# A new tail, split last stores and new places in a two-layer adjacency residual-norm kernel on one core

## Chip, core and metric

The kernel runs on one core of a Trainium2 chip. The metric is the device time of one execution in microseconds (us). Before the change it is 2085.56 us, the median of 3 runs (2084.93 to 2086.3). About 0.2% of it, 4.2 us, is what a measurement of this kernel can tell from no change.

## What is computed

There are 128 batches; each has x (128 x 512) and an adjacency matrix adj (128 x 128), all in float32. Two layers follow each other, and each ends in a residual and a layer norm.

```
# layer 0
agg = (adj @ x) / max(rowsum(adj), 1e-6)
x   = layernorm(x + relu(concat(x, agg) @ W.T))
# layer 1
Xw  = x @ Wv + bv;  sj, si = Xw @ aw[:d], Xw @ aw[d:]
A   = adj * exp(leaky_relu(sj[None, :] + si[:, None] + ab, 0.2))
T   = A / (rowsum(A) + 1e-12)
H   = sum over k = 0, 1, 2 of (T^k x) @ Wk[k] + bk[k]
x   = layernorm(x + relu(H))
```

## The kernel before

The 128 batches are worked in 32 groups of G = 4, first all groups in layer 0 (stage A), then all groups in layer 1 (stage B). The large products x @ W are made by a fast 2 x 2 block scheme with seven products in place of eight, with block sums of x and of the weights made beforehand.

**Chains and steps.** Every piece of TensorE work is a step of a chain, written as a name and a number.

- Stage A: chains P12, P56 and P74 (`pair`, line 305, seven steps of two 128x256 products each) and T (`last`, line 388, eleven steps: seven 128x256 products, then four 128x512 products with the turned adjacency).
- Stage B: chains O1, O2, O5, O6, O7, O4, O3 (`outer`, line 617, seven steps of one 128x385 product each) and C (`combine`, line 812). C has eight steps: for each batch b a `one(b)`, T times a 512-column row, and a `two(b)`, which adds T times another row on top. In C the steps are one(0), one(1), one(2), two(0), one(3), two(1), two(2), two(3).

A float32 product is two passes on TensorE. One `mm` (line 155) is one product. A step of a chain of seven usually waits on VectorE (DVE), ScalarE (ACT) or GpSimd (POOL) work that empties or refills a PSUM bank. For example step 3 (`prod(X, 6)`) is followed by DVE making W = X + s5 (line 637 in stage B), and step 5 (`prod(X, 7)`) writes X again and so must wait for that addition. In the T chain DVE lines 400 and 401 read what step T.2 left in the upper half of a bank, and T.3 writes the same bank.

**Order.** Two lanes of four PSUM banks each (bA0 to bA3, bB0 to bB3) hold two chains at a time. The order in which their steps alternate is written out by hand in strings: PA for a group of stage A, PT and PG for the passage from A to B, PB for a group of stage B, PL for the last group (lines 855 to 865). Everything else (loads, block sums on POOL, the turns `x_turn` at line 259 on DVE, layer norm, softmax pieces, stores) is put between the steps by tables PLACES_S, _A, _B, _M, _L and _T, which give each operation a position in half steps (lines 915 to 1027). Each engine runs its own instructions strictly in that order, so a waiting instruction holds up what is queued behind it on its engine. Nearly all DMAs are issued by SyncE (SP), in order too.

**Weights of the T matrix in stage B.** For all groups but the last, the 128x512 row of scores is sent through DRAM and turned. The last group is handled apart, so that nothing has to go to DRAM at the end:

- `t_scores` (line 721) makes dg, diagonal matrices of the scores, and `end_scores` (746) multiplies a matrix of ones by dg, takes the leaky relu and exp on ACT.
- `end_rows` (756): for each half h (two batches), DVE multiplies by the adjacency (760), and TensorE multiplies ones by T, a 128x256 product that leaves the row sums in every partition.
- `end_norm` (763): DVE adds epsilon (768), takes a 128x256 reciprocal (769) and multiplies T by it (770).
- The chain C of the last group: one(b) makes a product, DVE makes v1 from it in two additions (829, 830), ACT copies the addend of the second product into the same bank (831), two(b) multiplies on top, and DVE adds the residual (380).
- Layer norm of the last group: batches 0 and 1 by ACT squares and POOL (`end_mean`, `end_var`, `end_scales`), batches 2 and 3 by DVE `bn_stats` and POOL (`end_stats`, `end_rstd`); `end_apply` runs on ACT for batches 0 and 1, on DVE (565) for 2 and 3. `end_store` (569) has SP store each batch, 256 KB, in one DMA.

At the start, eight 128x512 products with the identity (lines 151 and 152) run on the eight banks while the first loads land.

Of the kernel before, what the change touches and what calls it, by code (L numbers as in the profile page):

```python
# [8 lines left out]
FP = mybir.dt.float32  # L9
# [7 lines left out]
def kernel(  # L17
# [41 lines left out]
    def need(*keys):  # L59
        for k in keys:  # L60
            assert k in done, k
# [89 lines left out]
    for t in bA + bB:  # L151
        nc.tensor.matmul(t, ident, ident[:, None, :].to_broadcast([P, Q, P]), start=True, stop=True)
# [414 lines left out]
    def end_store(b):  # L567
        need(("end_apply", b))
        nc.sync.dma_start(out[(NG - 1) * G + b], ys[2 * NG - 1, b // 2][:, b % 2])
# [186 lines left out]
    def end_rows(g, h):  # L756
        need(("end_scores", g), ("adj_turn",))
        T = TTs[g][:, 2 * h : 2 * h + 2].rearrange("p b n -> p (b n)")
        pt = lanes[0][1 + h][:, :FH]
        V.tensor_mul(T, T, adjs[2 * NG - 1][:, 2 * h : 2 * h + 2].rearrange("p b n -> p (b n)"))  # L760
        mm(pt, ones[:].to_broadcast([P, P]), T, True)

    def end_norm(g, h):
        need(("end_rows", g, h))
        T = TTs[g][:, 2 * h : 2 * h + 2].rearrange("p b n -> p (b n)")
        pt = lanes[0][1 + h][:, :FH]
        rr = halves()[:, :FH]
        V.tensor_scalar(rr, pt, ROW_EPS, None, ALU.add)
        V.reciprocal(rr, rr)  # L769
        V.tensor_mul(T, T, rr)  # L770
# [41 lines left out]
    def combine(lane, g):  # L812
        n = NG + g
        X, Y, W, Z = lane
        at_ = {0: X, 1: Z, 2: W, 3: Y}
# [8 lines left out]
        def one(b):  # L824
            need(("end_norm", g, b // 2) if g == NG - 1 else ("t_turn", g))
            need(("O4" if b > 1 else "O3", g, 7), ("sum_c", g, 0), ("sum_c", g, 1))
            mm(at_[b], TTs[g][:, b], row(b, 0, F, 0), True)
            v = v1[b] = v1s[(g * G + b) % 3]
            V.tensor_add(v[:, :258], at_[b][:, :258], row(b, F, 2 * BW, 0))
            V.tensor_add(v[:, 258:], at_[b][:, 258:], row(b, 0, 254, 1))  # L830
            L_.copy(at_[b], row(b, 254, 766, 1))  # L831

        def two(b):
            mm(at_[b], TTs[g][:, b], v1[b])
            late.append((residual, n, b, at_[b]))
# [15 lines left out]
    def step(lane, name, g, k):  # L851
# [3 lines left out]
    PA = "p74.5 P12.1 P12.2 p74.6 P12.3 p74.7 P12.4 t.1 P12.5 P12.6 t.2 P12.7 P56.1 t.3 P56.2 t.4 t.5 P56.3 t.6 t.7 t.8 t.9 t.10 t.11 P74.1 P74.2 P56.4 P56.5 P56.6 P74.3 P56.7 P74.4".split()  # L855
    PT = "p74.5 p74.6 O1.1 O1.2 O1.3 p74.7 O1.4 t.1 O1.5 O1.6 t.2 O1.7 O2.1 t.3 O2.2 t.4 t.5 O2.3 t.6 t.7 t.8 t.9 t.10 t.11 O2.4 O2.5 O2.6".split()
    PG = ("O5.1 O5.2 O5.3 O5.4 O2.5 O2.6 O6.1 O6.2 O5.5 O5.6 O5.7 O7.1 O6.3 O6.4 O7.2 "
          "O6.5 O2.7 O7.3 O6.6 O7.4 O6.7 O4.1 O4.2 O7.5 O4.3 O7.6 O7.7 O4.4 c.1 O4.5 "
          "O4.6 c.2 c.3 c.4 O4.7 O3.1 O3.2 O3.3 O3.4 c.5 c.6 c.7 c.8 O3.5 O3.6").split()
    PB = ("O1.1 o3.7 O1.2 O1.3 O2.1 O1.4 O1.5 O1.6 O2.2 O1.7 O2.3 O2.4 O5.1 O5.2 O2.5 O5.3 O2.6 O5.4 O2.7 "  # L860
          "O6.1 O5.5 O6.2 O5.6 O6.3 O5.7 O6.4 O7.1 O6.5 O6.6 O7.2 O7.3 O6.7 O4.1 O7.4 O7.5 O4.2 O4.3 O7.6 "
          "O4.4 O4.5 O7.7 c.1 O4.6 O4.7 O3.1 O3.2 c.2 O3.3 c.3 c.4 c.5 c.6 c.7 c.8 O3.4 O3.5 O3.6").split()
    PL = ("O1.1 o3.7 O1.2 O2.1 O1.3 O2.2 O1.4 O1.5 O1.6 O1.7 O2.3 O2.4 O5.1 O2.5 O5.2 O2.6 O2.7 O5.3 O5.4 O6.1 O5.5 O6.2 "
# [44 lines left out]
    def place_op(n, pos, name, m, *a):  # L908
# [3 lines left out]
        else:  # L912
# [3 lines left out]
        ("ln_apply", -2, 3): 4, ("ln_var", -2, 0): -9, ("sum_c22", -2): -40, ("ln_scales", -2): -1, ("ln_mean", -2): -15,  # L916
        ("ln_var", -2, 2): -4, ("load_y", -2, 1): -27, ("ln_apply", -2, 2): 10, ("ln_var", -2, 1): -4,
        ("load_y", -2, 0): -31, ("x_s4", -1): -36, ("ln_var", -2, 3): -12, ("x_s1", -1): -66, ("a_load", -2): -65,
        ("a_turn", -2): -36, ("x_s3", -1): -52, ("y_store", -2, 1): 25, ("ln_apply", -2, 1): 15, ("x_turn", 0, 0, 1): -20,
        ("y_store", -2, 0): 32, ("ln_apply", -2, 0): 15, ("load_left", 0, 0): -49, ("ln_apply", -1, 3): 68, ("x_s2", 0): 28,  # L920
        ("x_turn", 0, 1, 1): -37, ("load_adj", 0): 154, ("ln_var", -1, 0): 58, ("sum_c22", -1): 21, ("ln_scales", -1): 62,
        ("ln_mean", -1): 48, ("x_turn", 0, 0, 0): -28, ("ln_var", -1, 2): 55, ("load_y", -1, 1): 38, ("load_y", -1, 0): 40,
        ("ln_var", -1, 1): 55, ("ln_apply", -1, 2): 70, ("x_s1", 0): 5, ("x_turn", 0, 1, 0): -39, ("a_load", -1): 7,
        ("x_turn", 1, 0, 1): 55, ("x_inner", 0, 0): -12, ("a_norm", -1): -23, ("ln_var", -1, 3): 58, ("degree", -1): -48,
        ("a_turn", -1): 27, ("x_s3", 0): 19, ("y_store", -1, 1): 95, ("ln_apply", -1, 1): 79, ("x_inner", 0, 1): -29,
        ("y_store", -1, 0): 100, ("ln_apply", -1, 0): 82, ("load_left", 1, 0): 9, ("x_s1", 1): 97, ("x_turn", 1, 0, 0): 41,
        ("x_s2", 1): 99, ("x_s4", 0): 80, ("load_left", 1, 1): -24, ("x_inner", 1, 1): 61, ("x_turn", 1, 1, 0): 32,
        ("x_s3", 1): 127, ("x_inner", 1, 0): 64, ("x_turn", 1, 1, 1): 47, ("x_s2", -1): -44,
    }
    PLACES_A = {  # L930
        ("x_s4", 0): 35, ("ln_apply", 0, 3): 131, ("x_s2", 1): 86, ("x_turn", 1, 1, 1): 33, ("ln_var", 0, 0): 124,
        ("sum_c22", 0): 87, ("ln_scales", 0): 126, ("w_slot", 0, 1): 24, ("ln_mean", 0): 113, ("x_turn", 1, 0, 0): 33,
        ("ln_var", 0, 2): 124, ("load_y", 0, 1): 100, ("ln_var", 0, 1): 118, ("load_y", 0, 0): 100, ("ln_apply", 0, 2): 134,
        ("x_s1", 1): 67, ("x_turn", 1, 1, 0): 28, ("a_load", 0): 73, ("x_inner", 1, 0): 51, ("a_norm", 0): 36,
        ("ln_var", 0, 3): 115, ("degree", 0): 17, ("load_left", 2, 1): 38, ("w_slot", 0, 0): 4, ("a_turn", 0): 90,
        ("x_s3", 1): 83, ("y_store", 0, 1): 157, ("ln_apply", 0, 1): 140, ("x_turn", 1, 0, 1): 42, ("x_inner", 1, 1): 36,
        ("load_adj", 1): 37, ("y_store", 0, 0): 161, ("ln_apply", 0, 0): 138, ("load_left", 2, 0): 78,
    }
    PLACES_B = {
        ("t_norm", 0): 154, ("sum_r", 0, 1): 81, ("load_y", 0, 0): 170, ("ln_var", 0, 3): 230, ("x_turn", 1, 0, 1): 19,  # L940
        ("t_back", 0): 165, ("x_s1", 1): 66, ("ln_scales", 0): 239, ("t_sums", 0): 149, ("x_turn", 1, 1, 1): 19,
        ("load_left", 2, 0): 82, ("ln_var", 0, 1): 227, ("y_store", 0, 0): 264, ("t_turn", 0): 187, ("ln_var", 0, 2): 224,
        ("sum_c", 0, 0): 109, ("ln_apply", 0, 2): 273, ("ln_apply", 0, 3): 257, ("x_inner", 1, 1): 53, ("ln_var", 0, 0): 235,
        ("t_exp", 0): 140, ("load_left", 2, 1): 70, ("ln_apply", 0, 1): 257, ("y_store", 0, 1): 278, ("x_s2", 1): 68,
        ("x_turn", 1, 1, 0): -5, ("x_s3", 1): 97, ("ln_apply", 0, 0): 242, ("t_load", 0): 123, ("t_scores", 0): 119,
        ("x_turn", 1, 0, 0): 14, ("sum_r", 0, 0): 86, ("x_s4", 0): 42, ("load_adj", 0): 103, ("load_y", 0, 1): 190,
        ("ln_mean", 0): 223, ("sum_c", 0, 1): 115, ("x_inner", 1, 0): 41,
    }
    PLACES_M = {
        ("ln_mean",): 212, ("ln_apply", 3): 234, ("ln_var", 1): 219, ("ln_apply", 0): 250, ("y_store", 0): 251,  # L950
        ("ln_apply", 2): 231, ("ln_var", 2): 225, ("ln_apply", 1): 235, ("ln_var", 3): 225, ("ln_scales",): 230,
        ("y_store", 1): 244, ("ln_var", 0): 227,
    }
    PLACES_L = {
        ("end_store", 2): 158, ("sum_c", 1): 72, ("sum_r", 0): 71, ("end_store", 0): 158, ("t_scores",): 105,
        ("end_var", 1): 134, ("sum_r", 1): 71, ("load_adj",): 96, ("load_y", 0): 47, ("end_apply", 1): 160,
        ("load_y", 1): 106, ("end_mean", 1): 128, ("end_rows", 0): 111, ("end_mean", 0): 127, ("end_rstd", 2): 132,
        ("end_store", 1): 160, ("end_apply", 2): 137, ("end_stats", 2): 129, ("end_store", 3): 162, ("end_scales",): 140,
        ("sum_c", 0): 76, ("end_rstd", 3): 149, ("end_apply", 0): 144, ("end_scores",): 106, ("end_rows", 1): 111,
        ("end_norm", 0): 111, ("end_stats", 3): 138, ("end_norm", 1): 111, ("end_apply", 3): 158, ("adj_turn",): 96,  # L960
        ("end_var", 0): 131,
    }
    OPS = {f.__name__: f for f in (load_left, load_y, load_adj, x_turn, x_inner, x_s1, x_s2, x_s3, x_s4, sum_c22, degree, a_norm, a_load, a_turn, w_slot, ln_mean, ln_var, ln_scales, ln_apply, y_store, sum_r, sum_c, t_scores, t_load,
           t_exp, t_sums, t_norm, t_back, t_turn, end_scores, end_rows, end_norm)}
# [115 lines left out]
```

## Time and profile before

| | |
|---|---|
| median of 3 runs | 2085.56 us |
| the profiled execution's own time | 2083.08 us |
| its span, first to last instruction | 2081.3 us |
| TensorE matmul (PE), share of the span | 99% |
| TensorE weight loads (PEld), in parallel to PE | 64% |
| DVE / ACT / POOL | 73% / 56% / 66% |
| granted TensorE clock, mean | 0.998 |
| chain that ended last | 97% PE |
| DMA | 287.13 MB, mean 138 GB/s |

A line of the timeline is: start in us, length in us, engine, line, operation, out<-in with shapes, how many were merged (x), and in brackets how long the engine had been idle and who ended that. The wait table says which engine and line waited for which, in total us, times, and the longest. Ends of matmuls are modelled: a matmul's line is longer than the distance to the next, and a short stall shows only as a larger distance between starts.

### The profile page before, as it was taken

What the parts mean: (1) busy time and instruction counts of PE and PEld (TensorE: products, weight loads), DVE (VectorE), ACT (ScalarE), POOL (GpSimd) and SP (SyncE); (2) the same over time, 40 slices, a digit from 0 to 9 for tenths busy, and PEclk for the clock granted to TensorE, in tenths of its full rate; (3) what the DMA queues carried; (4) which work ended last, traced back from release to release, by engine and by line L of the source; (5) the groups of instructions that cost most, each with busy time, mean ns of one, the idle gap of its engine ahead of it and who ended that gap; (6) DMA issues with size and microseconds to landing.
All of it is one profiled execution on the core that took longest, in us unless ns stands there. A gap on an engine that the chain in (4) does not pass through costs nothing.

```text
span 2081.3 us, 25875 instructions
## 1 busy us (share of the span) xinstructions
PE 2062.5 (99%) x7096; PEld 1329.9 (64%) x7096; DVE 1525.8 (73%) x3414; ACT 1155.7 (56%) x2875; POOL 1377.7 (66%) x1263
## 2 busy tenths in 40 slices
PE   9999999999999999999999999999999999999997
PEld 6778888888878886555555555555555555555553
DVE  6777777777777777676776776776776776776766
ACT  2656666666666666355455455455455465465464
POOL 5877888887676776656656656656556556556552
PEclk9999999999999999999999999999999999999999
DMA  9776666666667776435434535535535435435423
GB/s 206 174 190 194 180 182 179 160 187 192 163 160 190 190 183 218 107 87 122 116 87 115 124 87 127 112 87 128 111 87 130 109 87 132 107 87 132 107 67 117
DMA packets 431070, 287.13 MB, mean 138 GB/s; under 512 B 155593, under 2 KB 353865, under 8 KB 430924
## 3 DMA queue, kind: packets, MB, share of 16 engines
q1 hardware_dynamic: 429996, 284.15, 54.6%
q10 hardware_dynamic: 800, 1.31, 0.3%
q8 instruction: 56, 0.92, 0.2%
q14 instruction: 90, 0.74, 0.1%
q0 software_dynamic: 128, 0.01, 0.0%
HBM read 191.60 MB, written 93.79 MB: 137 GB/s over the span
## 4 chain that ended last, share of the span: by engine, by line
PE 97%; DVE 1%; DMA 1%; ACT 0%; issue 0%; POOL 0%; SPq 0%; ACTq 0%; DVEq 0%
PE bA L155 51%; PE bB L155 46%; DMA yd<-y 0%; DMA xb<-in_x_dram 0%; DMA y<-in_x_dram 0%; PE bA L181 0%; DVE s L769 0%; DVE y L380 0%; POOL r L709 0%; ACT y L517 0%; DVE big L995 0%; DVE xl L259 0%; DVE xu L259 0%; DVE big L1003 0%; SPq L83 0%
## 5 line engine op out<-in xcount | busy, mean ns | idle before, releaser
L155 PE MATMUL bB<-big,xu 128*128 128x385 f32 (+1 forms) x1806 | 569.5, 435 | 1.0 <-DVE c L676 0.7
L155 PEld LDWEIGHTS bB<-big,xu 128*128 128x128 f32 x1806 | 339.4, 190 | 166.6 <-issue 30.1
L155 PE MATMUL bA<-big,xl 128*128 128x256 f32 (+1 forms) x1358 | 395.9, 416 | 0.3 <-DVE bA L475 0.3
L155 PE MATMUL bB<-big,xs 128*128 128x256 f32 (+1 forms) x1316 | 388.8, 416 | 0.0
L155 PEld LDWEIGHTS bA<-big,xl 128*128 128x128 f32 x1358 | 256.8, 189 | 100.1 <-issue 15.5
L155 PEld LDWEIGHTS bB<-big,xs 128*128 128x128 f32 x1316 | 249.5, 190 | 84.2 <-issue 1.7
L155 PE MATMUL bA<-big,xu 128*128 128x256 f32 (+1 forms) x896 | 290.0, 435 | 0.2
L155 PE MATMUL bA<-c,TT 128*128 128x512 f32 x512 | 245.9, 592 | 3.0 <-DVE c L669 1.9
L504 ACT ACTIVATE junk<-y,mv 128x512 bf16<-128x512 f32 x252 | 181.3, 719 | 72.7 <-POOL mv L499 68.5
L155 PEld LDWEIGHTS bA<-big,xu 128*128 128x128 f32 x896 | 165.4, 189 | 82.2 <-DVE bA L637 9.7
L517 ACT ACTIVATE y<-y,mv,rstd 128x512 f32<-128x512 f32 x252 | 201.5, 812 | 1.4 <-POOL mv L512 1.4
L380 DVE SCALAR_TENSOR_TENSOR y<-bA,y 128x512 f32<-128x512 f32 x256 | 170.4, 683 | 19.6 <-PE bA L155 13.4
L155 PE MATMUL bA<-big,xs 128*128 128x385 f32 x448 | 178.3, 492 | 0.0
L709 POOL TENSOR_TENSOR r<-r,s 128x770 f32<-128x770 f32 x64 | 115.1, 1820 | 86.4 <-DVE c L669 86.4
L155 PE MATMUL bB<-big,xl 128*128 128x385 f32 (+1 forms) x462 | 167.2, 480 | 0.5 <-ACT bA L456 0.4
L155 PEld LDWEIGHTS bA<-c,TT 128*128 128x128 f32 x512 | 96.8, 189 | 93.0 <-issue 48.1
L790 POOL TENSOR_TENSOR T<-ag,T 128x512 f32<-128x512 f32 x31 | 39.5, 1275 | 175.9 <-ACT T L785 175.9
L499 POOL TENSOR_SCALAR mv<-mv 128x4 f32<-128x4 f32 x63 | 14.5, 230 | 212.3 <-DVE y L380 212.3
L270 POOL TENSOR_TENSOR xs<-xl 128x896 f32<-128x896 f32 x63 | 131.4, 2086 | 23.9 <-PE bB L155 23.9
L282 POOL TENSOR_TENSOR xu<-xu,xs 128x896 f32<-128x896 f32 x63 | 131.8, 2091 | 8.8 <-PE bB L155 8.8
L831 ACT COPY bA<-r 128x512 f32<-128x512 f32 x64 | 37.7, 590 | 176.4 <-DVE big L830 170.7
L637 DVE TENSOR_TENSOR bB<-bB,s 128x385 f32<-128x385 f32 x128 | 72.5, 567 | 85.1 <-PE bB L155 75.4
(190 smaller groups left out, 3636.7 us busy)
## 6 DMA issues: line engine op xcount, KB each, us to landing
xb<-in_x_dram SPq DMA_DIRECT2D x256, 128.0 KB, 3.8
y<-in_x_dram SPq DMA_DIRECT2D x64, 512.0 KB, 4.3
yd<-y SPq DMA_DIRECT2D x64, 512.0 KB, 3.0
xb<-yd SPq DMA_DIRECT2D x256, 128.0 KB, 5.8
y<-yd SPq DMA_DIRECT2D x64, 512.0 KB, 5.9
out_dram<-y SPq DMA_DIRECT2D x62, 512.0 KB, 2.8
ag<-in_adj_dram SPq DMA_DIRECT2D x63, 256.0 KB, 5.9
sb<-sd SPq DMA_DIRECT2D x252, 64.0 KB, 3.2
```

The source lines that it names most:

```text
L155: nc.tensor.matmul(dst, lhsT, rhs, start=start, stop=True, skip_group_check=True)
L270: S_.tensor_add(xs[n][:, 0], xl[n][:, 0], xl[n][:, 1])
L282: S_.tensor_sub(xu[n][:, 1], xu[n][:, 1], xs[n][:, 1])
L380: V.scalar_tensor_tensor(y, t, 0.0, y, ALU.max, ALU.add, accum_out=mvs[n][:, b, 0:1])
L499: S_.tensor_scalar(mvs[n][:, :, 0], mvs[n][:, :, 0], -1.0 / F, None, ALU.mult)
L504: L_.activation(junk, ys[n, b // 2][:, b % 2], AF.Square, bias=mvs[n][:, b, 0:1], accum_out=mvs[n][:, b, 1:2])
L517: L_.activation(y, y, AF.Identity, bias=mvs[n][:, b, 0:1], scale=rstds[n][:, b : b + 1])
L637: V.tensor_add(W, X, s5)
L709: S_.tensor_add(r, r, s)
L790: S_.tensor_mul(T, adjs[NG + g], T)
L831: L_.copy(at_[b], row(b, 254, 766, 1))
```

## The change

Four things are changed. The new functions and the core of the diff:

```
-    for t in bA + bB:
+    for t in bA + bB[:3]:
...
     def end_store(b):
-        nc.sync.dma_start(out[(NG - 1) * G + b], ys[2 * NG - 1, b // 2][:, b % 2])
+        for p, eng in ((0, nc.sync), (1, nc.scalar)) if b > 1 else ((0, nc.sync),):
+            r = slice(p * P // 2, (p + 1) * P // 2) if b > 1 else slice(P)
+            eng.dma_start(out[(NG - 1) * G + b, r], ys[2 * NG - 1, b // 2][r, b % 2])
...
     def end_rows(g, h):
+        V.tensor_mul(t2, t2, adjs[2 * NG - 1][:, 2 * h : 2 * h + 2].rearrange("p b n -> p (b n)"))
+        for b in (2 * h, 2 * h + 1):
+            mm(pt[:, b : b + 1], T[:, b], ones, b == 0)
+    def end_recip(g, h):
+        need(("end_rows", g, 1))
+        t = lanes[0][0][:, 2 * h : 2 * h + 2]
+        V.tensor_scalar(rr, t, ROW_EPS, None, ALU.add)
+        V.reciprocal(rr, rr)
+        for b in (0, 1):
+            V.tensor_scalar(ends["dr"][:, 2 * h + b], ident, rr[:, b : b + 1], None, ALU.mult)
     def end_norm(g, h):
-        V.tensor_scalar(rr, pt, ROW_EPS, None, ALU.add)
-        V.reciprocal(rr, rr)
-        V.tensor_mul(T, T, rr)
+        pt = lanes[0][0][:, h * FH : (h + 1) * FH]
+        mm(pt, ones[:].to_broadcast([P, P]), ends["dr"][...], h == 0)
+        V.tensor_mul(T, T, pt)
+    def end_base(g, b):
+        t = (rs[NG + g], last22[g])[b // 2][:, b % 2].rearrange("p n m -> p (n m)")
+        mm(lanes[0][1 + b], ident, t[:, 254:766], True)
...
     def combine(lane, g):
+        if g == NG - 1:
+            to = {0: lanes[0][1], 1: lanes[0][2], 2: lanes[0][3], 3: X}
         def one(b):
-            L_.copy(at_[b], row(b, 254, 766, 1))
+            if g < NG - 1 or b == 3:
+                L_.copy(to[b], row(b, 254, 766, 1))
         def two(b):
-            mm(at_[b], TTs[g][:, b], v1[b])
+            mm(to[b], TTs[g][:, b], v1[b])
...
-    PA = "p74.5 P12.1 P12.2 p74.6 P12.3 p74.7 P12.4 t.1 P12.5 P12.6 t.2 P12.7 P56.1 t.3 P56.2 ... P74.1 P74.2 P56.4 ..."
+    PA = "p74.5 P12.1 p74.6 P12.2 P12.3 p74.7 t.1 P12.4 P12.5 t.2 P12.6 P12.7 P56.1 t.3 P56.2 ... P74.1 P56.4 P74.2 ..."
-    PB = "O1.1 o3.7 O1.2 O1.3 O2.1 ... O5.1 O5.2 O2.5 O5.3 O2.6 O5.4 O2.7 O6.1 O5.5 ... O3.1 O3.2 c.2 O3.3 c.3 c.4 c.5 c.6 c.7 c.8 O3.4 O3.5 O3.6"
+    PB = "O1.1 o3.7 O1.2 O1.3 O2.1 ... O5.1 O5.2 O2.5 O5.3 O2.6 O5.4 O5.5 O2.7 O6.1 ... O3.1 c.2 c.3 O3.2 c.4 c.5 c.6 O3.3 c.7 c.8 O3.4 O3.5 O3.6"
...
     PLACES_A
-        ("x_turn", 1, 1, 1): 33, ("x_turn", 1, 1, 0): 28, ("a_turn", 0): 90
+        ("x_turn", 1, 1, 1): 30, ("x_turn", 1, 1, 0): 26, ("a_turn", 0): 95
     PLACES_B
-        ("x_turn", 1, 0, 1): 19
+        ("x_turn", 1, 0, 1): 29
```

(In the strings p74, t, o3 and c are chains of the group before.)

1. The last group's softmax: row sums are made as 128x1 products, the reciprocal is taken of 128x2 numbers, spread over diagonal matrices dr (four 128x128 multiplies) and brought into all partitions by two 128x256 products of ones and dr.
2. The last group's combine: for batches 0 to 2 the addend of the second product is no longer copied by ACT; TensorE writes it beforehand with an identity product (`end_base`, three products of 512 columns) into banks bB1, bB0 and bB3, and two(b) adds to these banks. Batch 3 keeps the copy.
3. The stores of the last two batches are halved by partitions: SP issues the lower half, ACT the upper.
4. All orders and places are set anew: PA, PT, PG, PB and PL (PF, the first group, stays), and PLACES_S, _A, _B, _M, _L and _T, most entries by one to three half steps. The start table is unchanged. One of the eight identity products at the start is left out.

## The prediction

> **What bounds the kernel now.** I read the page's busy table and clock row first, then the wait table of TensorE, then the timeline of one group of each stage, and last the timeline of the tail.
>
> ```profile
> PE 2062.5 (99%) x7096; PEld 1329.9 (64%) x7096; DVE 1525.8 (73%) x3414; ACT 1155.7 (56%) x2875; POOL 1377.7 (66%) x1263
> ...
> PEclk9999999999999999999999999999999999999999
> ```
>
> PE is busy for 2062.5 of 2081.3 us at full clock, so the sum of the products cannot shrink; only PE's stalls, its start and the time after its last product can. The wait table (total, times, longest) shows little, and nearly all of it is in the last 30 us:
>
> ```profile
> PE bA L155 <- DVE c L669: 1.9, 1, 1.9
> PE bA L155 <- DVE TT L770: 1.0, 1, 1.0
> PE bB L155 <- DVE TT L760: 1.0, 1, 1.0
> PE bA L155 <- ACT bA L831: 0.8, 1, 0.8
> PE bB L155 <- DVE dg L730: 0.8, 1, 0.8
> ```
>
> Stalls below the modelled end of a product are not in it. They show in the distance between starts. A pass of 256 columns comes 0.216 us after the last one, of 385 columns 0.323, of 512 columns 0.429. In a group of stage A:
>
> ```profile
> 221.10 1.03 PE L155 MATMUL bB<-big,xs 128*128 128x256 f32 x4
> ...
> 221.55 0.41 DVE L401 TENSOR_TENSOR s<-bA,s 128x256 f32<-128x256 f32 x1
> ...
> 222.02 0.70 PE L155 MATMUL bA<-big,xu 128*128 128x256 f32 x2
> ...
> 222.56 1.03 PE L155 MATMUL bB<-big,xs 128*128 128x256 f32 x4
> ```
>
> P56.1 takes four passes, 0.86 us, so T.3 could start at 221.96. DVE line 401 ends just then, T.3 starts 0.05 late, and its two passes take 0.54 in place of 0.43: a wait that is met too late also delays the next weight load by 0.10. T.3 costs 0.155 us in each of 30 groups.
>
> Stage B has three such places per group: O3.7 (0.11, behind DVE 676), O5.1 (0.16, behind ACT's copy 626) and C.8:
>
> ```profile
> 1311.40 2.81 PE L155 MATMUL bA<-big,TT 128*128 128x512 f32 x6
> 1314.05 2.10 PE L155 MATMUL bB<-big,xu 128*128 128x385 f32 x6
> ```
>
> Six passes take 2.65 where 6 x 0.429 is 2.57: C.8's second weight load is 0.075 late, because ACT 831 ended only 0.08 before C.8 was due. Set side by side, these places give a rule of this trace: an input that ends 0.19 us or more ahead costs nothing (O1.5), one at 0.08 costs 0.075, one at 0.05 costs 0.10, one at 0 costs 0.155. So the cost is about 0.155 less the slack.
>
> **The change part by part.** The order of the changed program's instructions on each engine is known without a run; durations are those of the rows before.
>
> Stage A, T.3: three steps (T.2, P12.6, P12.7 then P56.1) take the place of T.2, P12.7, P56.1. T.3 comes one step, 0.86 us, later after T.2, and 400 and 401 now stand ahead of the degree's reductions on DVE. Its slack becomes 1.4 us: -0.155 x 30 = -4.65. What is late next: T.2, since T.1 has moved up. DVE's chain 320, 365, 366, 365, 366, 397 at their starts' distances (0.60, 0.45, 0.34, 0.45, 0.34) ends 397 0.21 us ahead of T.2. And T.7: line 409 now stands behind three turns (0.63 each) and ends 0.17 ahead. Both are above 0.155, so I take 0; 0.05 worse in each would give back 0.08 x 30 = 2.4.
>
> Stage B, C.8: one(3) now has O3.3 as well as C.6 and C.7 between it and C.8, 0.65 us more; slack 0.7; -0.075 x 30 = -2.25. O3.7 and O5.1 keep their distances and, counted instruction by instruction on DVE and ACT, their slack (0.04 and 0.06): no change.
>
> Stage B, O5.5, a new stall: the new PB puts O5.5 right after O5.4, two steps after O5.3, and the second xu turn has moved between O5.3's two DVE neighbours. Before:
>
> ```profile
> 1287.05 0.81 PE L155 MATMUL bA<-big,xs 128*128 128x385 f32 x2
> ...
> 1287.25 0.56 DVE L676 TENSOR_TENSOR c<-bB,c 128x385 f32<-128x385 f32 x1
> ...
> 1287.90 0.57 DVE L637 TENSOR_TENSOR bA<-bA,s 128x385 f32<-128x385 f32 x1
> ...
> 1315.44 0.70 DVE L259 STREAM_TRANSPOSE xl<-xb 128x512 f32<-128x512 f32 x1
> ...
> 1316.06 0.52 DVE L676 TENSOR_TENSOR r<-bB,r 128x385 f32<-128x385 f32 x1
> ```
>
> O5.3 starts at 1287.05, so O5.5 would be due three steps of 0.647 later, at 1288.99. On DVE 676 starts at 1287.25, the turn 0.45 to 0.53 after it, line 637 0.62 to 0.64 after that, at 1288.32 to 1288.42, and ends 0.56 later, at 1288.88 to 1288.98. Slack 0.01 to 0.11, cost 0.05 to 0.145; middle 0.10 x 30 groups = +3.0 (+1.5 to +4.4).
>
> Passage from A to B: the wait of O2.7 (0.86 + 0.10 at 826 us, behind DVE 676, which stood behind residuals waiting for y) goes, since 676 moves ahead of three of the four residuals. But O5.2, O5.3 and O5.5 now wait for banks that the later residuals read; counting DVE's queue from y's landing near 821 gives them 0.3, 1.0 and 0.35, against 0.2, 0 and 0.26 before. O4.7's 0.27 goes too. Sum near 0; +-1.5, because the landing (6.9 us after its issue before) is not known.
>
> Start: dropping an identity product (0.86) frees PE at 10.45, not 11.31, but FA.2 waits for DVE 995, which ends at 12.40 with both: 0. Cover gone, it would be worth 0.86.
>
> Tail, from O4.3 on (before: 2054.24). O4.4 fills PE to 2055.53; dg is ready at 2055.83 as before; scores 0.96, O4.5 to 2057.44, two identity products (0.86 each) to 2059.16. Meanwhile ACT's second exp ends at 2059.09 as before and line 760's second multiply at 2059.54. Four 128x1 products are eight passes; no row shows them, the nearest, 128x2 products at the start, come 0.112 apart: 0.9 (1.5 if the weight loads' own 0.19 sets the pace): 2060.05. O4.6 and the third identity product run to 2061.56. DVE: 128x2 add and reciprocal 0.2 each, two 128x128 multiplies 0.43 (dg's four took 0.86), O4.6's eviction, the second add, which the first ones-by-dr product awaits (same bank): 2061.8. It ends 2062.35, O4.7 2063.0; multiply by its result (0.42) to 2063.0; second product to 2063.55; then C.1 to C.8 without a stall, 8 x 0.86, the last starting at 2069.57. Before it started at 2071.51. As a sum: stalls of 6.2 us fall to 1.0, added products are 3 x 0.86 + 0.86: -1.8 to -1.9. What leaves is the reciprocal (1.75, twice) and ACT's copies:
>
> ```profile
> 2060.43 1.75 DVE L769 RECIPROCAL s<-s 128x256 f32<-128x256 f32 x1
> ```
>
> After PE: residual, `bn_stats`, POOL's 0.8 and line 565 keep their lengths and order, so the last 565 ends about 1.9 earlier, 2075.15. Stores:
>
> ```profile
> 2077.14 0.33 SPq L569 DMA_DIRECT2D out_dram<-y  x1
> 2077.57 0.40 SPq L569 DMA_DIRECT2D out_dram<-y  x1
> ```
>
> The last store's data were there at 2077.07, but it stood behind the one before it on SP: 0.45 lost. Landing takes 2.3. The Trainium skill's page "DMA: Bandwidth & Descriptors", section "Rules for kernel authors", speaks against the halves: transfers of disjoint partition halves serialize on the same 16 engines, and another issuing engine saves only issue time. By it the halves bring nothing in landing, at most the 0.45 in issue; had halving shortened the 2.3 in proportion, 1.1. Here SP's half of the last batch still stands behind batch 1's store, so I take 0.2 (0 to 0.6). Tail: -1.9 - 0.2 = -2.1 (-1.2 to -2.8).
>
> **Sum.** -4.65 - 2.25 + 3.0 + 0 + 0 - 2.1 = -6.0. From the profiled execution's 2083.08 that is 2077.1; it lies 2.5 below the median, so the prediction on the median is 2079.6.
>
> **Rivals.**
> - O5.5 costs nothing (the turn starts early enough, slack over 0.155): -9.0, 2076.6. For it: all estimates of that slack are within 0.1. Against: the row of the turn gives no start before 1287.70.
> - The gain is given back: T.2 and T.7 fall 0.05 below my count (+2.4), or the passage stalls 1.5 more while O5.5 costs its upper 4.4: -2 to -4, near 2082.6. For it: both slacks are 0.02 and 0.05 above the limit, and a place that costs 0.1 counts thirty times.
> - Slower: the xu turn in front of line 637 is itself made to wait (for its loads, or for DVE's turn), so that O5.5 misses by far more. From a cost of 0.30 per group (9.0/30) all is lost; from 0.44 it is slower by over 0.2%; at 0.5 it is +6, 2091.6. Against: its loads land 8 us or more ahead in the rows before.
> - The tail alone does what it says and the places nothing: -2.1, 2083.5; counted with the second.
>
> **How the numbers follow.** Forecast (-4.3 to -7.5, so 2078.1 to 2081.3) 0.46; O5.5 free 0.27; given back 0.22; slower 0.05. Faster by over 0.2% (4.2 us, what a measurement of this kernel can tell from no change) 0.73, within 0.22, slower 0.05. The range leaves out the slower case and the ends of the others: 2075.0 to 2084.0.
>
> **What would show it.** Right: PE's distances at T.3 become 0.43, C.8's 0.429; O5.5 shows 0.05 to 0.145; no 128x256 reciprocal; the last group's C.8 starts about 1.9 earlier counted from O4.3, and, with 3.9 from the stages (4.65 + 2.25 - 3.0), near 2065.7; the last DMA issue near 2071.6. Wrong: T.2, T.7 or another step stalls in every group, or O5.5 shows over 0.2 or 0.

## The result and the profile after

The changed kernel takes 2075.51 us in the median of 4 runs (2075.23 to 2075.95); before, measured beside it, took 2085.24 (2084.46 to 2086.3). The ratio is 0.9952, with a 95% interval of 0.9936 to 0.9967: 9.7 us less, where 6.0 was forecast. The profiled execution took 2075.23 us with a span of 2073.1.

The page's busy table and clock row have not changed in kind; TensorE is busy for 4.5 us less, though 12 more passes run, since a product that waits only a little counts as busy while it waits:

```profile
PE 2058.0 (99%) x7108; PEld 1334.0 (64%) x7108; DVE 1528.9 (74%) x3418; ACT 1158.7 (56%) x2872; POOL 1377.5 (66%) x1263
...
PEclk9999999999999999999999999999999999999999
```

The wait table of TensorE (total, times, longest) has lost the last group altogether. Lines 669, 770, 760 and 730 of before are gone; the 0.8 behind ACT's copy (851, before 831) is in the combine of group 30:

```profile
PE bA L152 <- POOL ident masks.py:199: 2.7, 1, 2.7
PE bA L155 <- DVE big L1017: 0.9, 1, 0.9
PE bA L155 <- ACT bA L851: 0.8, 1, 0.8
PE bB L155 <- ACT bA L456: 0.4, 1, 0.4
PE bA L155 <- DVE r L665: 0.4, 1, 0.4
```

In a group of stage A, DVE line 401 now ends 1.5 us ahead of T.3. T.3's two passes start at 221.05, and P56.2 follows 0.43 later (0.54 before, and 0.05 late on top). The next step in line is T.2: line 397 ends at 217.86, 0.14 ahead of it, and its two passes take 0.45 where 0.43 is free:

```profile
217.44 0.42 DVE L397 TENSOR_TENSOR bA<-bA,s 128x256 f32<-128x256 f32 x1
...
218.00 0.62 PE L155 MATMUL bA<-big,xu 128*128 128x256 f32 x2
...
218.46 1.89 PE L155 MATMUL bB<-big,xu 128*128 128x256 f32 x8
...
218.81 0.41 DVE L400 TENSOR_TENSOR s<-bA,s 128x256 f32<-128x256 f32 x1
219.14 0.41 DVE L401 TENSOR_TENSOR s<-bA,s 128x256 f32<-128x256 f32 x1
...
221.05 0.59 PE L155 MATMUL bA<-big,xu 128*128 128x256 f32 x2
...
221.48 1.03 PE L155 MATMUL bB<-big,xs 128*128 128x256 f32 x4
```

In stage B, C.7 and C.8 are free: three passes in 1.29, which is 3 x 0.429.

```profile
1345.46 1.45 PE L155 MATMUL bA<-big,TT 128*128 128x512 f32 x3
1346.75 2.10 PE L155 MATMUL bB<-big,xu 128*128 128x385 f32 x6
```

And O5.5 has the new stall. The turn (259) stands between lines 678 and 639; 639 ends at 1321.61, O5.5 is due at 1321.72, and the four passes of O5.4 and O5.5 take 1.35 where 4 x 0.323 is 1.29:

```profile
1319.98 0.56 DVE L678 TENSOR_TENSOR c<-bB,c 128x385 f32<-128x385 f32 x1
...
1320.45 0.70 DVE L259 STREAM_TRANSPOSE xu<-xb 128x512 f32<-128x512 f32 x1
...
1321.07 1.51 PE L155 MATMUL bA<-big,xs 128*128 128x385 f32 x4
...
1321.08 0.53 DVE L639 TENSOR_TENSOR bA<-bA,s 128x385 f32<-128x385 f32 x1
...
1322.42 0.49 PE L155 MATMUL bB<-big,xu 128*128 128x385 f32 x1
```

In the tail, the reciprocal of 128 x 2 numbers takes a tenth of the one it replaces (1.75):

```profile
2053.64 0.17 DVE L771 RECIPROCAL rr<-rr 128x2 f32<-128x2 f32 x1
```

TensorE's starts of marked steps cut both profiled executions into stretches (us). Each row of the experiments below can be set against this table.

| from | to | before | changed | difference |
|---|---|---|---|---|
| start | P12.1 of group 3 | 88.74 | 88.35 | -0.39 |
| there (stage A) | P12.1 of group 31 | 692.89 | 689.59 | -3.30 |
| there (passage) | O1.1 of group 1 | 67.15 | 64.74 | -2.41 |
| there (stage B) | O1.1 of group 31 | 1167.66 | 1167.17 | -0.49 |
| there | O4.3 of group 31 | 37.81 | 37.58 | -0.23 |
| there (new softmax, combine) | C.8 of group 31 | 17.27 | 15.30 | -1.97 |
| there | end of the span | 9.80 | 10.41 | +0.61 |

The sum is -8.2; the reported times of the two profiled executions differ by 2083.08 - 2075.23 = 7.85. But the medians differ by 9.7. So nearly 2 us lie outside what these two traces show; where, the experiments had to find.

### The profile page after: what moved, and what is told of

It reads as the page before. It is cut to its first block, busy times and chain, and to the rows that moved or that the text cites. A ratio compares the mean times of both kernels' runs of the same rounds, so it can differ in the third digit from the quotient of the medians.

```text
span 2073.1 us, 25956 instructions
## 1 busy us (share of the span) xinstructions
PE 2058.0 (99%) x7108; PEld 1334.0 (64%) x7108; DVE 1528.9 (74%) x3418; ACT 1158.7 (56%) x2872; POOL 1377.5 (66%) x1263
## 3 DMA queue, kind: packets, MB, share of 16 engines
q10 hardware_dynamic: 960, 1.57, 0.4%
## 4 chain that ended last, share of the span: by engine, by line
PE 58%; DVE 0%; POOL 0%; ACT 0%; issue 0%; ACTq 0%
PE bA L155 31%; PE bB L155 27%; POOL r L711 0%; DVE r L671 0%; ACT y L562 0%; POOL rs L539 0%; DVE dg L732 0%; DVE y L380 0%; DVE st L546 0%; ACT bA L851 0%; POOL rs L555 0%; DVE r L675 0%; ACT s L636 0%; DVE big L849 0%; DVE big L848 0%
## 5 line engine op out<-in xcount | busy, mean ns | idle before, releaser
L155 PE MATMUL bA<-big,xl 128*128 128x256 f32 (+1 forms) x1358 | 406.1, 416 | 0.3 <-DVE bA L475 0.3
L155 PE MATMUL bA<-c,TT 128*128 128x512 f32 x512 | 241.0, 592 | 0.0
L155 PE MATMUL bB<-big,xl 128*128 128x385 f32 (+1 forms) x462 | 172.0, 480 | 0.4 <-ACT bA L456 0.4
L671 DVE TENSOR_TENSOR r<-bB,r 128x385 f32<-128x385 f32 x192 | 106.5, 555 | 43.6 <-PE bB L155 40.0
```

Source lines behind the costliest of these rows:

```text
L155: nc.tensor.matmul(dst, lhsT, rhs, start=start, stop=True, skip_group_check=True)
L671: V.tensor_add(part(dst, b, BW), t, part(src, b, BW))
```

## Experiments

The theory at the start was the prediction's: every stage keeps its own stalls, and the sum of the stages is the change. The first four kernels are before with one part of the change each.

**Stage A alone.** Only the order `PA` and the table of stage A:

```
-    PA = "p74.5 P12.1 P12.2 p74.6 P12.3 p74.7 P12.4 t.1 ..."
+    PA = "p74.5 P12.1 p74.6 P12.2 P12.3 p74.7 t.1 P12.4 ..."
-    PLACES_A = { (before) }
+    PLACES_A = { (changed kernel) }
```

> Before, with only the order PA and the places of stage A of the change. Theory (each stage keeps its own gain, and they add): T.3 runs without a stall (28 x 0.155 = 4.3 gained), T.2 gives back what the changed kernel's trace shows (0.9), nothing moves elsewhere: 3.4 less than before, from group 3 to group 31 of stage A 3.3 less. Rival (the gain is lost in the passage, because the loads and layer norms of the last groups are placed against the old passage): the stretch of stage A 3.3 shorter, but the passage to stage B longer by 1 to 3, so 0.5 to 2.4 less than before.

Measured: 2082.54 (2079.96 to 2086.02, 18 runs) against 2085.0 (52 runs), ratio 0.9989 (0.9982 to 0.9996), 2.5 less. Its trace has stage A at 689.60, 3.29 shorter, and the passage at 68.73, 1.58 longer: P74.1 of group 31 now waits 1.4 us for DVE's residual (380). The rival holds: the places of the last groups of stage A are set for one order, and the old ones do not fit the new order.

**Stage B alone.** Only `PB` and the table of stage B:

```
-    PB = ("O1.1 o3.7 O1.2 O1.3 O2.1 O1.4 O1.5 O1.6 O2.2 ..."
+    PB = ("O1.1 o3.7 O1.2 O1.3 O2.1 O1.4 O1.5 O2.2 O1.6 ..."
-    PLACES_B = { (before) }
+    PLACES_B = { (changed kernel) }
```

> Before, with only the order PB and the places of stage B of the change. Theory: C.8 without its 0.075 (-2.1), O5.5 with 0.055 (+1.6), O3.7 and O5.1 as they were: 0.5 less, no change that can be measured. Rival of the prediction's count: O5.5 costs 0.10 per group, +0.8 in all. Rival (before's executions outside the profile are 2 us longer because of something in stage B, which the new places end): 2 or more less in the median, though the trace shows 0.5.

Measured: 2084.23 (13 runs), ratio 0.9995 (0.9987 to 1.0003). In its trace C.8's 29 x 0.075 are gone, O5.5 has 29 x 0.054 = 1.57, O3.7 and O5.1 have what they had (0.10 and 0.16); stage B is 1.02 shorter, half of it in the first groups. The theory holds; O5.5's cost is the lower end of the prediction's count.

**The passage alone.** Only `PT`, `PG` and the tables `PLACES_S`, `PLACES_M`, `PLACES_T`:

```
-    PT = "p74.5 p74.6 O1.1 O1.2 O1.3 p74.7 O1.4 t.1 ..."
+    PT = "p74.5 p74.6 O1.1 O1.2 O1.3 p74.7 t.1 O1.4 ..."
...
-    PLACES_S = { (before) }
+    PLACES_S = { (changed kernel) }
```

> Before, with only PT, PG and the places of the passage and of the weight loads beside it (PLACES_S, PLACES_M, PLACES_T). Theory: the stalls of the passage (O2.7, O4.7, T.4, O5.7) go by themselves, 1.9 to 2.4 less than before. Rival: they went only because stage A's new order brings the passage's y and residuals in another rhythm; then 0 to 1 less, with the wait of O2.7 or another of 0.5 or more still there.

Measured: 2084.65 (13 runs), ratio 0.9998 (0.9990 to 1.0006): nothing that can be told from none. The wait of O2.7 is gone and the passage is 1.20 shorter, but T.2 of group 30 waits 0.36, O5.3 still 0.37, and in group 1 of stage B O1.5 waits 1.6. Neither side had it whole: the passage's own waits do go by themselves, but the gain is handed on to the neighbour whose places still fit the old one.

**The last group alone.** The new softmax, combine, `PL` and `PLACES_L`, with whole stores:

```
+    def end_recip(g, h):
...
+    def end_base(g, b):
...
-    PL = ("O1.1 o3.7 O1.2 O2.1 ..."
+    PL = ("O1.1 o3.7 O1.2 O1.3 ..."
```

> Before, with only the last group's new softmax, combine, PL and PLACES_L; whole stores by SyncE as before. Theory: PE's last product starts 1.9 to 2.2 earlier, and without the halves the end keeps all of it: 1.9 to 2.2 less than before; the end after the last product as before (last 565 to the end of the span 4.2). Rival (what is lost behind PE's last product, 0.6 in the changed kernel, comes of the new order of the last layer norm and not of the halves): 1.4 to 1.6 less, with 4.7 from the last 565 to the end.

Measured: 2081.55 (2081.02 to 2082.05, 19 runs), ratio 0.9984 (0.9977 to 0.9990): 3.5 less, though its trace shows the 1.97 of the changed kernel from O4.3 to C.8 (15.30) and nothing more. More telling than the median is the spread: 1.0 us over 19 runs, where before's 52 runs beside it spread over 3.9 (2083.14 to 2087.07). So the old last group costs a varying amount, and the new one does not.

The traces of the first two show what it is. The stretch from O4.3 to C.8, the same code in both as in before, took 19.62 in the kernel with stage A alone and 18.54 with stage B alone, against 17.27 in before's profile. TensorE in the kernel with stage A alone:

```profile
2060.94 1.13 PE L155 MATMUL bA<-c,TT 128*128 128x512 f32 x2 [1.04 <-DVE TT L770]
2063.99 3.78 PE L155 MATMUL bA<-c,TT 128*128 128x512 f32 x4 [1.93 <-DVE c L669]
2067.57 1.92 PE L155 MATMUL bA<-big,TT 128*128 128x512 f32 x2
```

Six passes behind the long wait come 0.85 apart, not 0.43. A table of stretches gives the reason (length; busy time of PE, PEld, DVE, ACT, POOL with their counts; granted clock; DMA share; GB/s). In the kernel with stage A alone, the 3.41 us ahead of the fall of the clock, and the time at the lower clock:

```profile
2059.54:2062.95 3.41, 1.49 (x4) 0.30 (x2) 3.34 (x4) 0.19 (x2) 1.43 (x3) 1.00 0.00 0
2062.95:2069.78 6.83, 5.79 (x7) 2.52 (x8) 3.85 (x11) 3.05 (x5) 0.00 (x0) 0.50 0.00 1
```

The same with stage B alone:

```profile
2061.49:2064.90 3.41, 1.37 (x3) 0.55 (x4) 3.34 (x6) 0.00 (x0) 0.50 (x2) 1.00 0.00 0
2064.90:2068.31 3.41, 3.41 (x5) 1.33 (x5) 1.62 (x6) 1.93 (x3) 0.00 (x0) 0.50 0.00 0
```

And before, where the clock does not fall until the last product is done:

```profile
2060.90:2064.31 3.41, 1.88 (x5) 0.43 (x3) 3.34 (x4) 0.59 (x2) 1.43 (x3) 1.00 0.00 0
2064.31:2067.73 3.42, 1.98 (x4) 0.68 (x4) 3.23 (x8) 0.55 (x2) 0.00 (x0) 1.00 0.00 0
```

The clock stayed at 0.50 for 6.83 us in the one and for 3.41 in the other, two stretches and one. The next falls, behind the last product, come at 2076.61 and 2075.14, 6.83 after the rise in both. So in these traces the clock changes only at points that lie 3.41 us apart, and the points lie elsewhere in each execution (those of before are counted back from its fall at 2074.55). Where TensorE was busy for 1.49 or 1.37 of the 3.41 us between two points, the clock fell. In the three traces of the old last group in which it did not, the emptiest stretch between two points had 1.88 (before), 1.67 (the passage alone) and 1.89 (all places, below). By these traces the sum of the waits in one stretch counts, and chance decides how the stretches cut the waits. Moved over before's own timeline, about three quarters of all positions of the points leave a stretch with 1.5 or less: an estimate of the share of executions that lose.

So before's profile was a lucky execution, and the runs agree. Of before's 52 runs here, the 12 with a mean clock of 0.997 took 2085.43 to 2087.07, the 33 with 0.998 took 2083.38 to 2085.49, the 7 with 0.999 took 2083.14 to 2083.69. This mean is a rough guide only: it counts the end of the span too, where the clock is at 0.50 in every trace, and before's profile itself has 0.998.

**Filling the waits.** So the new theory is that the last group's stalls themselves bring the clock down. The direct test leaves every wait where it is and only gives TensorE something to do in it:

```
         for f, b in ((one, 0), (one, 1), ...
-            f(b)
+            fill = g == NG - 1 and f is one and b == 0
+            for k in range(3 * fill):
+                if k == 1:
+                    f(b)
+                nc.tensor.matmul(lanes[0][3], ident, ident[:, None, :].to_broadcast([P, Q, P]), start=True, stop=True)
+            if not fill:
+                f(b)
             yield
```

> Before, with three idle identity products of 512 columns put into the waits of the last group's combine: one ahead of C.1, two behind it, where TensorE stands still for 1.20 and 2.09 us. They write a bank that nobody reads any more; what is computed stays. They take away no wait. Theory (the stalls of the last group, 5.4 us in 11, let the granted clock fall to 0.50 for 3 to 7 us in most executions, and before's profile showed one where it did not): TensorE is busy through the stalls, the clock stays at 1.00, the stretch from O4.3 to C.8 takes 17.3 +- 0.2; median 2083.2, 1.8 less than before, and the spread between executions falls from 4 us to 1.5 or less, though three products are added. Rival (the clock falls for a reason that has nothing to do with the stalls, or the spread comes from the transfers): 2085.0 and a spread of 4 as before.

Measured: 2083.03 (2082.57 to 2083.45, 13 runs) against 2084.5 (2083.22 to 2085.52, 17 runs), ratio 0.9992 (0.9984 to 1.0000). In the trace the stretch takes 17.28, with the clock at 1.00 throughout:

```profile
2063.00:2066.00 3.00, 2.79 (x7) 1.01 (x7) 2.93 (x5) 0.00 (x0) 0.19 (x1) 1.00 0.00 0
2066.00:2069.00 3.00, 2.89 (x7) 1.10 (x7) 2.37 (x7) 1.76 (x4) 0.00 (x0) 1.00 0.01 3
```

Three products that compute nothing make the kernel 1.5 us faster in the median, with an interval that just reaches no change; the spread falls from 2.3 to 0.9, as the theory said. The clock of this one trace proves little, since it stayed at 1.00 in before's profile too. How empty TensorE gets says more. In each of the five traces with the old last group unfilled, the emptiest 3.41 us, wherever they are laid, hold 1.13 us of busy time; here they hold 2.42, with the new last group 2.60:

```profile
2062.30:2065.71 3.41, 1.13 (x2) 0.30 (x2) 3.34 (x6) 0.00 (x0) 0.78 (x2) 1.00 0.00 0
```

(This is before.) So with the waits filled no position of the stretches brings TensorE near the 1.37 and 1.49 that were followed by a fall. The theory stands, the rival has fallen: the waits cost what they last, and a second time through the clock, by an amount that differs from execution to execution.

Here a rule can be set behind the rows. The Trainium skill's page "TensorE: Matmul & The Clock Gate", section "HAM oscillation — how this bites in real kernels", asks that TensorE have no idle gaps of more than about 3.4 us. By that rule the old last group is safe, since its longest wait is 2.09, and the loss is 0. By the rows, stalls of 0.95, 1.15, 1.20 and 2.09 within 11 us already halved the clock. The page's other statement, in Part 1 on the clock gate, that activity is judged over a free-running window of 3.4 us, agrees with what is seen: drops of 3.41 and 6.83 us that began at different points.

**Whole stores.** The changed kernel with before's stores:

```
-        for p, eng in ((0, nc.sync), (1, nc.scalar)) if b > 1 else ((0, nc.sync),):
...
+        nc.sync.dma_start(out[(NG - 1) * G + b], ys[2 * NG - 1, b // 2][:, b % 2])
```

> The changed kernel, with the last two batches stored whole by SyncE as before. Theory (the halves cost time: from the last line 565 to the end of the span 4.70 with them, 4.23 without): 0.4 to 0.5 less than the changed kernel, 2075.0. Rival of the prediction (the halves save 0.2): 2075.7. Rival (the order of the last layer norm, not the halves, makes the end longer): 2075.5, with 10.4 from the last C.8 to the end of the span.

Measured: 2074.8 (2074.59 to 2075.12, 5 runs), below every one of the changed kernel's four (2075.23 to 2075.95), 0.7 in the median. But those four were measured at another time, when before's median was 0.7 higher too (2085.24 against 2084.5). The traces are firmer: from C.8 to the end of the span, the three kernels with the new last group and halves (the changed one, the next one and the three places below) take 10.39 to 10.41, and the three with whole stores by SyncE (the last group alone, this one, the three places with whole stores) take 9.95 to 10.09. The halves lose 0.3 to 0.5. The DMA issues of the last 8 us fit this (size of one, and median us from issue to landing). In the changed kernel, then in before:

```profile
out_dram<-y SPq DMA_DIRECT2D x2, 256.0 KB, 2.2
out_dram<-y SPq DMA_DIRECT2D x2, 128.0 KB
out_dram<-y ACTq DMA_DIRECT2D x2, 128.0 KB, 2.8
```

```profile
out_dram<-y SPq DMA_DIRECT2D x4, 256.0 KB, 2.3
```

ScalarE's halves of 128 KB land later after their issue than a whole of 256 KB (the landing of SyncE's halves is not in the trace), and SyncE's half of batch 3 is issued at 2068.92, behind batch 1's store at 2068.52.

**The eighth identity product.**

```
-    for t in bA + bB[:3]:
+    for t in bA + bB:
```

> The changed kernel with the eighth identity product at the start put back. Theory of the prediction (FA.2 waits for DVE line 995 in any case, which hides 0.86): no change, 2075.5 +- 0.3, P12.1 of group 3 at 88.4 +- 0.4. Rival (the product's 0.86 is on the path): 2076.2 to 2076.4. Rival (without it the clock comes up later): less than the changed kernel.

Measured: 2075.77 (2075.57 to 2076.15, 5 runs), 0.26 more in the median, with overlapping runs. Its profiled execution began late (P12.1 of group 3 at 89.19), but that start lies between 88.35 and 89.10 in the other kernels up to here with one code or the other. No 0.86 is seen: it is hidden, as forecast; 0.3 could not be told from nothing.

**The three places that were left.** The traces leave three stalls per group in stage B: O3.7 (0.10), O5.1 (0.16) and O5.5 (0.055). Each is a step's DVE or ACT neighbour with something queued ahead of it that could stand behind it:

```
-        ("x_turn", 1, 1, 0): -5     ("x_turn", 1, 0, 1): 29
+        ("x_turn", 1, 1, 0): 2      ("x_turn", 1, 0, 1): 34
-        ("ln_scales", 0): 242       ("ln_apply", 0, 0): 242
+        ("ln_scales", 0): 240       ("ln_apply", 0, 0): 241
```

> The changed kernel with four more places in stage B: the xl turn (1,1,0) from -5 to 2, behind the DVE line 678 that O3.7 waits for; the xu turn (1,0,1) from 29 to 34, behind the line 639 that O5.5 waits for; and the layer norm's line 517 of batch 0 (with its POOL scales ahead of it, 242 to 240 and 241) ahead of the copy 636, so that it no longer stands ahead of the bias copy 628 that O5.1 waits for. Theory (a stall of these places is only what DVE and ACT have queued ahead, by the rule cost = 0.155 less the slack): O3.7 29 x 0.104, O5.5 29 x 0.055 and of O5.1 half to all of 29 x 0.16 go: 3.0 + 1.6 + 2.3 to 4.6 = 7 to 9 less than the changed kernel, 2066.5 to 2068.5. Rival (the turns or line 517 are themselves late where they are now, or POOL and the loads behind them are pushed): another step of each group stalls in their place, 2 to 6 less, 2069.5 to 2073.5.

Measured: 2066.17 (2065.89 to 2066.36, 4 runs), ratio to before 0.9911 (0.9897 to 0.9924): 9.3 less than the changed kernel. Stage B takes 1157.67, 9.5 less, and none of the three steps stalls. O5.4 and O5.5 in this kernel:

```profile
1317.14 0.57 DVE L639 TENSOR_TENSOR bA<-bA,s 128x385 f32<-128x385 f32 x1
...
1317.58 1.46 PE L155 MATMUL bA<-big,xs 128*128 128x385 f32 x4
...
1318.26 0.70 DVE L259 STREAM_TRANSPOSE xu<-xb 128x512 f32<-128x512 f32 x1
1318.88 0.48 PE L155 MATMUL bB<-big,xu 128*128 128x385 f32 x1
```

Line 639 comes straight behind 678, the turn after both, and the four passes take 1.30. The theory's upper end holds.

**All places, old last group.** Stage A, stage B and the passage together, in before:

```
 PA, PT, PG, PB, PLACES_A, PLACES_B, PLACES_S, PLACES_M, PLACES_T: as in the changed kernel
 end_rows, end_norm, combine, end_store, PL, PLACES_L: as before
```

> Before with all three sets of places that ran singly (stage A, stage B, passage with the weight loads) at once, and the old last group: no new softmax, combine or stores. Theory (the places of the passage, of stage A and of stage B belong together: the losses of the single runs, 1.6 in the passage with A alone and 1.4 in group 1 of stage B with the passage alone, are gone): the passage from P12.1 of group 31 to O1.1 of group 1 takes 64.7 as in the changed kernel, the single stages as there; with the old last group's 17.3 at full clock 2076.5, with its usual loss of clock 2078.0 to 2079.0 in the median, and a spread of 3 to 4. Rival (the three add as they ran singly, 2.5 + 0.8 + 0.4): 2081.3.

Measured: 2078.88 (2077.11 to 2081.03, 7 runs) against 2084.8, ratio 0.9973 (0.9962 to 0.9984). In its trace the passage takes 64.74 and stage A 689.61, as in the changed kernel. Singly the three gave 2.5, 0.8 and 0.4, together 5.9. The interval of the median, 3.3 to 7.9, still holds the 3.7 of plain addition; the trace decides against it, since neither the 1.6 of the passage nor the 1.6 in group 1 of stage B is there. And the spread of 3.9 is back with the old last group.

**The halves again, and two more waits.** First, the kernel of the three places with whole stores:

```
 end_store as in the whole stores above
```

> The kernel of e8_places with whole stores by SyncE in place of the halves. Theory (the halves cost 0.3 to 0.7 as in e6_whole_stores, whatever the stages do): 2065.5 +- 0.3. Rival (no difference): 2066.2.

Measured: 2065.7 (2065.22 to 2066.18, 4 runs), 0.47 less in the median than with halves, with overlapping runs; from C.8 to the end the trace has 10.08 against 10.39. The ratio to before is 0.9909 (0.9895 to 0.9922). Then, from there:

```
-        nc.sync.dma_start(out[(NG - 1) * G + b], ...
+        (nc.scalar if b == 3 else nc.sync).dma_start(out[(NG - 1) * G + b], ...
-          ... O7.7 O3.1 O3.2 O3.3 O3.4 c.1 c.2 c.3 c.4
+          ... O7.7 O3.1 O3.2 c.1 O3.3 O3.4 c.2 c.3 c.4
```

> The kernel of e10_places_whole with two more moves: the last batch's whole store is issued by ScalarE, so that it no longer stands behind batch 1's on SyncE; and in PL the step C.1 of group 30 stands ahead of O3.3, so that DVE's additions for C.4 come before line 675 (673 in this kernel), which waits for POOL. Theory: C.3 to C.4 loses its 0.96, and the last store is issued 0.4 earlier, 1.2 to 1.4 less than e10: 2064.2. Rival (issue is not what ends last[...], so the end of the span stays): 0.9 less, 2064.6. Rival (the later O3.3 holds up the last group's own chain): no gain from C.1.

Measured: 2065.25 (2064.73 to 2065.94, 4 runs), ratio to before 0.9906 (0.9891 to 0.9921), the best of all, but only 0.45 below the last one. C.3 to C.4 has lost its 0.96: from O1.1 to O4.3 of group 31 the trace shows 36.57, where it was 37.57. The store by ScalarE brings nothing: it is issued 0.03 after the last line 565 ends, where SyncE alone was 0.51 behind, but the end comes 10.21 after C.8, with SyncE alone 10.08. The profiled execution is the slowest of the four; in it the passage took 66.16, 1.4 more than in its neighbour: y's two loads were issued at 812.36 and 815.20 and landed at 817.29 and 820.62, where in the changed kernel they landed at 815.28 and 817.70, and O5.2, O5.3 and O5.5 waited for what stands behind the residuals:

```profile
819.87 1.78 PE L155 MATMUL bA<-big,xs 128*128 128x385 f32 x4
821.49 0.81 PE L155 MATMUL bB<-big,xu 128*128 128x385 f32 x2
822.97 1.24 PE L155 MATMUL bA<-big,xs 128*128 128x385 f32 x3 [0.67 <-ACT bA L628]
```

## Why the prediction was right and wrong

The time lies within the range, though only 0.5 from its lower end, and the direction was right; the size was 6.0 where 9.7 came. That the stretches of the traces, -8.2, lie only 2.2 from the sum is in part luck: stage A fell 1.35 short and the end 0.8, while stage B and the passage gave 1.2 and 2.4 more than was forecast. By the prediction's own terms:

- **T.3**, forecast -4.65: right. It runs free, which is 28 x 0.155 = 4.3 between groups 3 and 31. What is late next was named rightly, T.2, but taken at 0: it costs 0.93 in all, 0.02 in each group, since line 397 ends 0.14 ahead of it and not the 0.21 that was counted, and 0.36 more in one. T.7, the other one named, costs 0.10 once. Stage A gained 3.30. The rival's 0.05 a group was too much, 0 too little.
- **C.8**, forecast -2.25: right (29 x 0.075 = 2.2 gone).
- **O5.5**, forecast +3.0: right in mechanism and mis-sized. It is 0.055 per group, +1.6, where the count ran from 0.05 to 0.145 and the middle was taken. Line 639 takes 0.53 behind the turn, not the 0.56 of a row where it came after a pause, and started at the early end of the count. A slack of 0.11 and a stall of 0.055 fit the rule of 0.155 less the slack.
- **O3.7 and O5.1**, forecast unchanged: right (0.104 and 0.16 per group in both).
- **The passage**, forecast 0 +- 1.5: wrong, -2.4. The failed step is the landing of y, counted "from y's landing near 821". In the changed kernel y landed at 815.28 and 817.70, 11.9 and 14.3 after O1.1 of group 0, where before it was 13.7 and 16.1. With y 1.8 earlier the residuals did not hold up O5.2, O5.3 and O5.5. Where y did land late, in the last experiment's profile, those very steps stalled, by 1.3 together. The stalls were forecast rightly, for a landing that the changed kernel's own profile does not have.
- **The start**, forecast 0: right within the 0.8 by which starts vary (88.35 to 89.19).
- **The tail to C.8**, forecast -1.8 to -1.9 at full clock: right, -1.97.
- **The stores**, forecast -0.2: wrong in sign. With the same last group the halves end 0.3 to 0.5 later than whole stores. The end after C.8 is 0.6 longer than in before's profile, but the six traces with the old last group vary there from 9.80 to 10.37, so the rest is not shown. The rule quoted in the prediction, that halves land no faster, was the right one to listen to; what it left as a gain, the 0.45 of issue, was not to be had: SyncE's half stood behind batch 1's store, and the last experiment, which issued the last store 0.48 sooner after line 565, ended no earlier.
- **From the profile to the median**: the other large miss, 1.9. "It lies 2.5 below the median, so the prediction on the median is 2079.6" takes the gap between the profiled execution and the others for a constant. It was the old last group's loss of clock, which that one execution escaped and the change abolishes. With 7.85 from the traces, the rest of 1.9 is about what the filled waits gave back (1.5, with three products more) and what before's executions at the mean clock of 0.997 and 0.998 lose against those at 0.999. The prediction had the stalls before it, 6.2 us in the last 30, and priced them only at what they lasted.

The rival in which O5.5 costs nothing came nearest in time (2076.6), for a reason that is not its own: O5.5 did cost. Given back and slower did not occur. What stays open: the exact limit below which the clock falls, since no run varied the length of the wait. The stretches in the last group place it between 1.49 and 1.67 of 3.41 us, but ends of matmuls are modelled, and behind the last product one stretch with 1.42 (the eighth identity product) was not followed by a fall. Open too is why y's loads land at different times from execution to execution.

## What to carry to other kernels

When one profiled execution is faster than all the others, ask what it escaped before using it as the base of a sum; the spread between executions is itself a reading, and here it pointed to one stretch of 17 us. A wait on a nearly full TensorE can cost twice, by its length and by the clock behind it, so idle products in an unavoidable wait can pay. And in a queue written out by hand look at what stands ahead of the one instruction a step waits for: four operations moved by a few places gave 9.3 us, nearly as much as the whole change, while parts of a plan that were set together gave 3.7 us singly and 5.9 together in the medians.

## What the runs showed of the hardware that was not expected

Stalls of 0.95, 1.15, 1.20 and 2.09 us within 11 us took the granted clock to 0.50 for 3.41 or 6.83 us in two of five traces, after a stretch of 3.41 us in which TensorE was busy for 1.37 or 1.49; with identity products in the waits no such stretch had less than 2.42. Halves of a 256 KB store that ScalarE issued took 2.8 us to land, a whole one by SyncE 2.2 to 2.3. A DVE instruction of 128x385 took 0.52 to 0.53 directly behind a turn and 0.54 to 0.57 otherwise; a reciprocal of 128x2 took 0.17, one of 128x256 took 1.75.
